# Mix of a spectral layer: block stores on GpSimd's queue, weights alone on SyncE's, part of x loaded later, first spectrum loaded in two parts

## The chip, the cores and the metric

The kernel runs on one core of a Trainium2 chip. The metric is the device time of one execution in microseconds (us). The core has five engines that run their own instruction streams: TensorE (PE, with its weight loads as PEld), VectorE (DVE), ScalarE (ACT), GpSimd (POOL) and SyncE (SP). SP only issues transfers here; ACT and POOL issue some too. All transfers are moved by the core's 16 DMA engines.

## The reference, cut to what matters

The input x is 8 images of 32 channels and 256 by 256 points, in float32. Four layers follow one another, each added to its normalised input: a spectral convolution, a 5 by 5 convolution, a gated recurrence over the columns, and directional running maxima with a 1 by 1 mix. The change concerns the first layer and the start of the second:

```python
x_ft = jnp.fft.rfft2(x)
out_lo = jnp.einsum('bixy,ioxy->boxy', x_ft[:, :, :M1H, :M2H], w1)
out_hi = jnp.einsum('bixy,ioxy->boxy', x_ft[:, :, -M1H:, :M2H], w2)
...
out = jnp.fft.irfft2(out_ft, s=(h, w))
return out + bias
...
x = x + _L0_conv_ref(_gn(x), ...)
x = x + _L1_conv_ref(_gn(x), L1_conv_kernel, 1, 2)
```

Only 32 row frequencies at each end and 32 column frequencies are kept. Each kept mode has its own complex 32 by 32 matrix between channels; multiplying by it is called the Mix here.

## The kernel before, in words

The program has four stages in order of time: `forward_and_mix` (forward transform to 212 us, Mix to about 273 us), `inverse_and_conv` (to about 956 us), `recurrence` (to about 2410 us) and `maxima_and_mix` (to the end). The order of instructions on each engine is the order in which the program writes them; nothing reorders them.

**Mix.** The loop runs over eight blocks q of four row modes each (`NQ` = 8, `KC` = 4). A block uses two weight tiles of 1 MB (c = 0, 1). There are sixteen such loads in all; they use seven buffers (`AHEAD` = 7), so the first seven are loaded during the forward transform and each of the other nine is issued on SP after the half block that frees its buffer (`load_weights`, L109). Per block TensorE does 128 matmuls into PSUM (`mp`, L285, four buffers for each half s), and ACT (s = 0, L298) and DVE (s = 1, L296) copy them into a stage tile `sm`, two buffers for each half. Each block is then stored to a DRAM scratch `smd` by eight DMAs of 64 KB (L307), issued in turn by SP and POOL. In block q = 5, ahead of that block's stores on SP, the six loads of `xb` for the first unit are issued (call at L302, DMA at L323): three parts i of three column tiles each, two channels halves, 768 KB each.

**Waits on the queues.** SP and POOL issue in order. A DMA signals its landing on one of eight semaphores, taken in turn: SP and ACT share eight, POOL has eight of its own. Before a semaphore is used again the DMA that used it last must have landed, so at most eight are in flight for each set.

**Inverse transform and convolution.** A unit is one image and half its channels. `load_spectrum(b)` reads the modes of image b back from `smd` into `spec`: partitions 0 to 63 as stored (L391), 64 to 127 with real and imaginary parts exchanged (L393, two DMAs). For image 0 these three go out on SP, ACT and POOL; image 1's follow on SP; images 2 to 7 are loaded by ACT during the convolution. One part of the exchanged half is negated (image 0: `half`, ACT at L649, 64 partitions x 1024; image 1: DVE at L398; the later ones: POOL). `means` (L404) and `spectrum` (L411 to L421, a chain of small DVE operations) correct the mean. Then `over_rows` does the row matmuls (`tp`, L442, copied by ACT at L449), `over_columns` the column matmuls (`up`, L459), and DVE adds the input `xb` (L468) to give `x1`. A unit has nine column tiles p; p = 0 to 2 use part 0 of `xb`, 3 to 5 part 1, 6 to 8 part 2. The parts of the next unit are loaded by POOL as each part has been used. The 5 by 5 convolution (`vp`, L530) works in place on `x1`, which is stored to `x2d` by twelve DMAs on SP per channel group (L586 to L593). The recurrence reads `x2d`; its first column block is loaded into `first` by POOL and normalised into `xn`.

**Memory.** Tile pools are laid one behind the other from the left, or from the right with `side="right"`. `xb` is in `a2x` on the right; `spec` is in `a2f`, the first pool of `inverse_and_conv` on the left. A new tile waits for the last users of the bytes that it takes over.

Of the kernel before, what the change touches and what calls it, by code (L numbers as in the profile page):

```python
# [9 lines left out]
F32 = mybir.dt.float32  # L10
AF = mybir.ActivationFunctionType
# [5 lines left out]
P = 128  # L17
B, C, H, W = 8, 32, 256, 256
NG = 16
KM = 32  # L20
# [4 lines left out]
Q = H // A  # L25
# [54 lines left out]
def forward_and_mix(tc, k, d, smd, xmean, keep):  # L80
# [4 lines left out]
    nc = tc.nc  # L85
    CH = 4
    NK = C // CH
    HB = H // 32
    KC = 4
    AHEAD = 7  # L90
    SLICES = 4
    HW = float(H * W)
    with ExitStack() as ctx:
# [19 lines left out]
        with ExitStack() as inner:  # L113
# [8 lines left out]
            xs, ys, sps, squares, turned = {}, {}, {}, {}, {}  # L122
# [144 lines left out]
                nc.vector.tensor_copy(xmean, xm)  # L267

        xp2 = keep.enter_context(tc.tile_pool(name="a2x", bufs=1, side="right", reuse_waits="tile"))
        xb = conv_x(nc, d, xp2)  # L270
        sp = ctx.enter_context(tc.tile_pool(name="ms", bufs=2, reuse_waits="tile"))
        ps = ctx.enter_context(tc.tile_pool(name="mp", bufs=4, space=PSUM))
        with tc.manual_schedule(engines=None):
            for q in range(NQ):
                stage = [sp.tile([P, KC, KY, C], F32, name=f"sm_{q}_{s}", tag=f"sm{s}") for s in range(2)]
                for c in range(2):
                    wt = wts.pop(2 * q + c)
                    for i in range(0, KY // 2, 4):
                        mps = [ps.tile([P, 4, KC, C], F32, name=f"mp_{q}_{c}_{i}_{s}", tag=f"mp{s}") for s in range(2)]
                        for y in range(4):  # L280
                            for h in range(2):
                                for s in range(2):
                                    r, to = slice(64 * s, 64 * s + 64), slice(64 * h, 64 * h + 64)
                                    ky = KY * h + KY // 2 * c + i + y
                                    nc.tensor.matmul(  # L285
                                        mps[s][to, y].rearrange("p j o -> p (j o)"),
                                        lhsT=xf[r, ky, q].rearrange("p r b x -> p (r b x)"),
                                        rhs=wt[r, h, i + y].rearrange("p j o -> p (j o)"),
                                        start=True,
                                        stop=True,  # L290
                                    )
# [12 lines left out]

                for s in range(2):
                    for m in range(KC):
                        (nc.sync, nc.gpsimd)[m % 2].dma_start(  # L307
                            out=smd[s, KC * q + m].rearrange("h r b y o -> (h r b) (y o)"),
                            in_=stage[s][m::KC, m].rearrange("p y o -> p (y o)"),
                        )  # L310

    return xb


def conv_x(nc, d, pool):
    CH = 8
    parts = {}

    def load(u, b, h, i, queue):
        lo, hi = 3 * i, 3 * i + 3  # L320
        for ch in range(2):
            t = pool.tile([P, hi - lo, CH, Q], F32, name=f"xb_{u}_{ch}_{i}", tag=f"xb{ch}{i}")
            queue.dma_start(  # L323
                out=t.rearrange("p t c q -> p (t c q)"), in_=d["xl"][b, 2 * h + ch, :, lo * CH * Q : hi * CH * Q]
            )
            for p in range(lo, hi):
                parts[u, ch, p] = t[:, p - lo]

    load.parts = parts
    return load  # L330


# [1 line left out]
    return x2d[b, lo:hi].rearrange("w a c q -> (a c) w q")  # L334


def inverse_and_conv(tc, k, d, smd, xmean, x2d, stb, first, xb):

# [5 lines left out]
    nc = tc.nc  # L344
    CH = 8
# [6 lines left out]
    PLACES = (1, 2, 3, 5, 6, 7, 8)  # L352
    FIRST = (1, 3, 4, 7)
    with ExitStack() as ctx:
        spp = ctx.enter_context(tc.tile_pool(name="a2f", bufs=2, reuse_waits="tile"))
        wk = ctx.enter_context(tc.tile_pool(name="a2w", bufs=2, reuse_waits="tile"))
        one = ctx.enter_context(tc.tile_pool(name="a2c", bufs=1, reuse_waits="tile"))
        sm = ctx.enter_context(tc.tile_pool(name="a2s", bufs=3, reuse_waits="tile"))
        ps = ctx.enter_context(tc.tile_pool(name="a2p", bufs=1, space=PSUM))

        bias = k.bias
# [8 lines left out]
        xs, specs, state = xb.parts, {}, {}  # L370

        def x1_of(u, ch):
            return x1s[(2 * u + ch) % 5][0]
# [10 lines left out]

        def load_spectrum(b):

            t = spp.tile([P, 2, 2, KM // 2, C], F32, name=f"spec_{b}", tag="spec")
            queues = (nc.sync, nc.scalar, nc.gpsimd) if b == 0 else 3 * (nc.scalar if b > 1 else nc.sync,)
            modes = smd[:, :, :, :, b].rearrange("s x h r y o -> (s x) h r (y o)")
            flat = t.rearrange("p h r y o -> p h r (y o)")  # L390
            queues[0].dma_start(out=flat[0:64].rearrange("p h r n -> p (h r) n"), in_=modes.rearrange("p h r n -> p (h r) n"))  # L391
            for ro in range(2):
                queues[ro + 1].dma_start(out=flat[64:128, :, ro], in_=modes[:, :, 1 - ro])  # L393
            specs[b] = t

        def turn(b, engine):
            t = specs[b]
# [245 lines left out]

        n = len(units)
        with tc.manual_schedule(engines=None):
            load_spectrum(0)
            load_spectrum(1)
            half = specs[0][64:128, :, 1]
            nc.scalar.activation(half, half, AF.Copy, scale=-1.0)  # L649
            spectrum(0, means(0))  # L650
            for u in range(2):
                begin(u)
# [553 lines left out]
@with_exitstack  # L1206
def kernel(ctx: ExitStack, tc: tile.TileContext, d: dict, out: bass.AP):
    pool = ctx.enter_context(tc.tile_pool(name="const", bufs=1))
    dram = ctx.enter_context(tc.tile_pool(name="scratch", bufs=1, space=DRAM))
    k = load_consts(tc, pool, d)  # L1210
    xmean = pool.tile([P, B, NG], F32, name="xmean")
    mean1 = pool.tile([P, B], F32, name="mean1")
    mv3 = pool.tile([P, B, 2], F32, name="mv3")
    loaded = recurrence_weights(tc, pool, d)
    keep = ExitStack()
    smd = dram.tile([2, KM, 2, 2, B, KM // 2, C], F32, name="smd")
    x2d = dram.tile([B, W, A, C, Q], F32, name="x2d")
    x3d = dram.tile([W // 8, P, A, 2, 8 * Q], F32, name="x3d")
    fwd = dram.tile([W // 8, P, A, 2, 8 * Q], F32, name="fwd")
    xb = forward_and_mix(tc, k, d, smd, xmean, keep)  # L1220
# [4 lines left out]
    inverse_and_conv(tc, k, d, smd, xmean, x2d, stb, first, xb)  # L1225
# [124 lines left out]
```

## Time and profile before

| | us |
|---|---|
| runs shown | 2980.09, 2985.53, 2977.58 |
| median | 2980.09 |
| profiled execution, its own time | 2983.02 |
| profiled execution, span | 2981.2 |
| forward transform, 0 to 212 | 212 |
| Mix to the first spectrum's load, 212 to 273.5 | 61.5 |
| load of the first spectrum to the first row matmul | about 9 |
| inverse transform and convolution | about 673 |
| recurrence | about 1454 |
| maxima and mix | about 571 |

In the profile, times are counted from the start of the span. A row of the chain of waits or of the timeline gives start, duration and what ran, with the line of the kernel; "x4" means four instructions merged. `SPq`, `ACTq` and `POOLq` are the engines' issuing parts. "DMA smd<-sm" in the chain is a wait until such a transfer landed. In a row of one tile, "536/537/589" are the shortest, median and longest duration in ns. Over the whole span TensorE is busy 93%, DVE 86%, ACT 63%, POOL 30%.

### The profile page before, as it was taken

The numbers are of one execution on the slowest core, as the hardware profiler recorded it, in microseconds if no ns is written. First come the engines' busy times: TensorE is split into PE (matmuls) and PEld (weight loads), VectorE is DVE, ScalarE is ACT, GpSimd is POOL, SyncE is SP. The second block draws the span as 40 slices with busy tenths as digits, with TensorE's granted clock in tenths as the row PEclk, the third lists the DMA queues.
The fourth block names the chain that finished last, engine by engine and source line by source line (L and its number), as shares of the span: only waits on it lengthen the run. The fifth ranks groups of instructions, "written<-read, shape, count | busy, mean of one in ns | idle before, by whom it ended". The sixth has DMA issues, their size and how long they took to land.

```text
span 2981.2 us, 109664 instructions
## 1 busy us (share of the span) xinstructions
PE 2763.3 (93%) x46712; PEld 1633.7 (55%) x46712; DVE 2572.6 (86%) x5130; ACT 1888.7 (63%) x4469; POOL 885.0 (30%) x1266
## 2 busy tenths in 40 slices
PE   8985999999998999999999999999999588888887
PEld 4663454444444666666666666666666233333333
DVE  5762888888887799999999999999999999999998
ACT  4552677677766788888888888888887222222222
POOL 0012111222212555555555555555555200000000
PEclk9997999999999999999999999999999799999998
DMA  9987677777765766676667666766674698888885
GB/s 396 364 308 254 216 228 229 223 232 229 235 220 150 153 144 140 149 172 145 140 146 172 147 141 145 169 153 139 142 168 117 210 376 324 326 324 323 327 337 229
DMA packets 426331, 651.38 MB, mean 218 GB/s; under 512 B 279249, under 2 KB 283233, under 8 KB 399089
## 3 DMA queue, kind: packets, MB, share of 16 engines
q1 hardware_dynamic: 397760, 488.68, 57.2%
q0 software_dynamic: 14928, 75.72, 7.4%
q10 hardware_dynamic: 13152, 79.96, 7.0%
q8 instruction: 366, 6.00, 0.8%
q14 instruction: 125, 1.02, 0.1%
HBM read 371.63 MB, written 272.63 MB: 216 GB/s over the span
## 4 chain that ended last, share of the span: by engine, by line
PE 71%; DVE 20%; DMA 3%; issue 2%; ACT 1%; SPq 1%; POOL 0%; ACTq 0%; DVEq 0%; POOLq 0%
PE r L815 14%; PE z L815 13%; PE vp L530 13%; PE ni L815 7%; PE nh L815 6%; PE up L459 5%; DVE rv L1101 4%; PE yp L142 3%; DVE dq L1116 3%; DVE uq L1118 2%; PE tp L442 2%; DVE m L1127 2%; DVE m L1124 2%; DVE m L1121 2%; PE sp L169 2%
## 5 line engine op out<-in xcount | busy, mean ns | idle before, releaser
L823 PE MATMUL z<-hs,weights 64*64 64x256 f32 x4080 | 538.8, 382 | 0.0
L907 POOL TENSOR_TENSOR xw<-xw,hs 128x256 f32<-128x256 f32 x496 | 339.6, 685 | 633.4 <-DVE hs L906 630.2
L823 PE MATMUL ni<-hs,weights 64*64 64x256 f32 x4080 | 524.9, 375 | 0.0
L823 PE MATMUL r<-hs,weights 64*64 64x256 f32 x4080 | 524.9, 375 | 0.0
L1159 ACT ACTIVATE ot<-o,bres 128x512 f32<-128x512 f32 x256 | 154.9, 688 | 492.1 <-PE o L1133 477.1
L563 DVE SCALAR_TENSOR_TENSOR x<-vp,r,x 128x128 f32<-128x128 f32 (+2 forms) x640 | 350.4, 562 | 96.6 <-PE vp L530 85.6
L530 PE MATMUL vp<-x,c_conv 64*64 64x384 f32 (+5 forms) x4608 | 422.7, 491 | 0.4 <-DVE x L563 0.4
L897 ACT ACTIVATE n<-n,bih 128x256 f32<-128x256 f32 x510 | 259.2, 508 | 183.9 <-DVE n L896 183.9
L899 POOL TENSOR_TENSOR a<-zm,xn 128x256 f32<-128x256 f32 x510 | 372.5, 730 | 3.4 <-ACT zm L892 3.3
L815 PE MATMUL r<-hs,weights 64*64 64x256 f32 x2040 | 319.1, 389 | 1.4 <-DVE hs L906 0.2
L815 PE MATMUL z<-xn,weights 64*64 64x256 f32 x2040 | 305.6, 376 | 9.9 <-ACT xn L795 9.9
L530 PEld LDWEIGHTS vp<-x,c_conv 64*64 64x64 f32 x4608 | 222.3, 132 | 167.8 <-issue 88.9
L1133 PE MATMUL o<-m,wsc 32*32 32x512 f32 x3072 | 224.6, 712 | 95.9 <-DVE m L1127 94.8
L815 PE MATMUL nh<-xn,weights 64*64 64x256 f32 x2040 | 305.7, 377 | 0.0
L815 PE MATMUL r<-xn,weights 64*64 64x256 f32 x2040 | 305.5, 376 | 0.0
L815 PE MATMUL z<-hs,weights 64*64 64x256 f32 x2040 | 305.2, 376 | 0.0
L815 PE MATMUL ni<-hs,weights 64*64 64x256 f32 x2040 | 304.8, 375 | 0.0
L795 ACT ACTIVATE xn<-xw,shift,turned 128x256 f32<-128x256 f32 x492 | 288.5, 586 | 0.0
L823 PEld LDWEIGHTS ni<-hs,weights 64*64 64x64 f32 x4080 | 284.7, 133 | 0.3
L891 DVE SCALAR_TENSOR_TENSOR n<-nh,bhh,rs 128x256 f32<-128x256 f32 x510 | 246.1, 483 | 42.9 <-ACT rs L890 28.9
L823 PEld LDWEIGHTS r<-hs,weights 64*64 64x64 f32 x4080 | 281.1, 131 | 0.2
L890 ACT ACTIVATE rs<-r,brz 128x256 f32<-128x256 f32 x510 | 241.3, 473 | 58.6 <-PE r L823 38.0
(176 smaller groups left out, 6230.5 us busy)
## 6 DMA issues: line engine op xcount, KB each, us to landing
xb<-in_xl_dram POOLq DMA_DIRECT2D x90, 768.0 KB, 7.1
xa<-in_xt_dram SPq DMA_DIRECT2D x64, 1024.0 KB
fwd<-fm SPq DMA_DIRECT2D x256, 256.0 KB
out_dram<-ot ACTq DMA_DIRECT2D x64, 1024.0 KB
xw<-x2d SPq DMA_DIRECT2D x248, 256.0 KB
fw<-fwd SPq DMA_DIRECT2D x31, 2048.0 KB
x3d<-xw SPq DMA_DIRECT2D x240, 256.0 KB
x<-x3d SPq DMA_DIRECT2D x30, 2048.0 KB
```

The source lines that it names most:

```text
L530: ins = nc.tensor.matmul(vps[bank][to, :, dst], lhsT=k.conv[r, P : P + 64] if kind == 2 else k.conv[r, o], rhs=pair_of(u, ch, g, lo, hi, s ...
L563: nc.vector.scalar_tensor_tensor(x, src[o], r1[rows, g : g + 1], x, ALU.mult, ALU.add, accum_out=s1[rows, 0, n, ch, g : g + 1])
L795: nc.scalar.activation(norms[bi][:, b, w], raws[bi][:, b, w], AF.Identity, bias=shift[:, b : b + 1], scale=sc[:, 1, b : b + 1])
L815: ins = nc.tensor.matmul(out[r], lhsT=weights[r, kind, gate, :], rhs=src[r], start=start, stop=stop)
L823: ins = nc.tensor.matmul(out[pairs[1 - i]], lhsT=weights[r, kind, gate, :], rhs=prev[r, :, q0 : q0 + Q], start=False, stop=stop,)
L890: rs = nc.scalar.activation(r, p["r"], AF.Sigmoid, bias=brz[:, 0:1])
L891: nc.vector.scalar_tensor_tensor(m, p["nh"], bhh[:, 2:3], r, ALU.add, ALU.mult)
L897: nc.scalar.activation(m, m, AF.Tanh, bias=bih[:, 2:3])
L899: product = nc.gpsimd.tensor_tensor(a, zm, cur, ALU.mult)
L907: nc.gpsimd.tensor_tensor(raw, raw, new, ALU.add)
L1133: nc.tensor.matmul(banks[bi][b2][i][32 * j : 32 * j + 32].rearrange("p (w q) -> p w q", q=Q), lhsT=wsc[q, b2, t, :], rhs=src[j][q, b2], st ...
L1159: nc.scalar.activation(ot[:, i], banks[bi][b2][i], AF.Identity, bias=bres[:, b2, i : i + 1])
```

## The change

All stores of blocks 0 to 6 are issued by POOL. Those of the last block go to SP, POOL, ACT and SP by row mode. `xb`'s part 0 alone is loaded in the Mix, by SP in block q = 6; part 1 is loaded by POOL behind the late spectrum, part 2 by POOL at the start of `inverse_and_conv`, from a pool of its own (`a2y`). The spectrum's pool moves to the right side, and a function `spectra` loads a chosen range of row modes of one half s with three DMAs. For image 0 the first 24 of 32 modes (`EARLY`) are loaded by SP in block 6, ahead of that block's stores in the program; the other eight after the last block, as stored on SP, exchanged on POOL. Every later image takes six DMAs, three for each half, where it took three. The negation of image 0 is done half by ACT, half by DVE, and DVE's half stands ahead of the `spectrum` chain. In `inverse_and_conv`, `load(0, 2)` (part 2 of `xb`) stands ahead of image 1's spectrum.

```diff
-        xb = conv_x(nc, d, xp2)
+        xb = conv_x(nc, d, [xp2, xp2, None])
+        spp = keep.enter_context(tc.tile_pool(name="a2f", bufs=2, side="right", reuse_waits="tile"))
+        spectrum_of = spectra(nc, smd, spp)
+        EARLY = slice(0, KC * (NQ - 2))
...
-                if AHEAD + 2 * q in (2 * NQ, 2 * NQ + 1):
-                    for i in range(3):
-                        xb(0, 0, 0, i, nc.sync)
+                if q == NQ - 2:
+                    xb(0, 0, 0, 0, nc.sync)
+                    for early in range(2):
+                        spectrum_of(0, early, EARLY, (nc.sync,))
+                queues = 4 * (nc.gpsimd,) if q < NQ - 1 else (nc.sync, nc.gpsimd, nc.scalar, nc.sync)
                 for s in range(2):
                     for m in range(KC):
-                        (nc.sync, nc.gpsimd)[m % 2].dma_start(
+                        queues[m].dma_start(
...
+            for late in range(2):
+                spectrum_of(0, late, slice(EARLY.stop, KM), (nc.sync, nc.gpsimd))
+            xb(0, 0, 0, 1, nc.gpsimd)
+
+    return xb, spectrum_of
+
+
+def spectra(nc, smd, pool):
+    tiles = {}
+
+    def load(b, s, x, queues):
...
+        if b not in tiles:
+            tiles[b] = pool.tile([P, 2, 2, KM // 2, C], F32, name=f"spec_{b}", tag="spec")
+        modes = smd[s, x, :, :, b].rearrange("x h r y o -> x h r (y o)")
+        flat = tiles[b].rearrange("p h r y o -> p h r (y o)")
+        own, other = (slice(64 * i + KM * s + x.start, 64 * i + KM * s + x.stop) for i in range(2))
+        queues[0].dma_start(out=flat[own].rearrange("p h r n -> p (h r) n"), in_=modes.rearrange("p h r n -> p (h r) n"))
+        for ro in range(2):
+            queues[-1].dma_start(out=flat[other, :, ro], in_=modes[:, :, 1 - ro])
...
-            t = pool.tile([P, hi - lo, CH, Q], F32, name=f"xb_{u}_{ch}_{i}", tag=f"xb{ch}{i}")
+            t = pools[i].tile([P, hi - lo, CH, Q], F32, name=f"xb_{u}_{ch}_{i}", tag=f"xb{ch}{i}")
...
-        spp = ctx.enter_context(tc.tile_pool(name="a2f", bufs=2, reuse_waits="tile"))
...
+        xb.pools[2] = ctx.enter_context(tc.tile_pool(name="a2y", bufs=1, reuse_waits="tile"))
...
-            t = spp.tile([P, 2, 2, KM // 2, C], F32, name=f"spec_{b}", tag="spec")
-            queues = (nc.sync, nc.scalar, nc.gpsimd) if b == 0 else 3 * (nc.scalar if b > 1 else nc.sync,)
...
+            queue = nc.scalar if b > 1 else nc.sync
+            for s in range(2):
+                spectrum_of(b, s, slice(0, KM), (queue,))
...
-            load_spectrum(0)
+            load(0, 2)
             load_spectrum(1)
-            half = specs[0][64:128, :, 1]
-            nc.scalar.activation(half, half, AF.Copy, scale=-1.0)
+            for y in range(2):
+                half = specs[0][64:128, y, 1]
+                if y:
+                    nc.vector.tensor_scalar_mul(half, half, -1.0)
+                else:
+                    nc.scalar.activation(half, half, AF.Copy, scale=-1.0)
             spectrum(0, means(0))
```

More of the change, by code (lines that the diff above doesn't have):

```diff
@@ L310, in forward_and_mix, with conv_x @@
                         )
-    return xb
-def conv_x(nc, d, pool):
+            for late in range(2):
[13 more added lines that the diff above has]
+            queues[-1].dma_start(out=flat[other, :, ro], in_=modes[:, :, 1 - ro])
+    load.tiles = tiles
+    return load
+def conv_x(nc, d, pools):
     CH = 8
@@ L327, in load @@
                 parts[u, ch, p] = t[:, p - lo]
-    load.parts = parts
+    load.parts, load.pools = parts, pools
     return load
@@ L334, in columns, with inverse_and_conv @@
     return x2d[b, lo:hi].rearrange("w a c q -> (a c) w q")
-def inverse_and_conv(tc, k, d, smd, xmean, x2d, stb, first, xb):
+def inverse_and_conv(tc, k, d, xmean, x2d, stb, first, xb, spectrum_of):
     nc = tc.nc
@@ L369, in inverse_and_conv @@
         units = [(b, h) for b in range(B) for h in range(C // (2 * CH))]
-        xs, specs, state = xb.parts, {}, {}
+        xs, specs, state = xb.parts, spectrum_of.tiles, {}
         def x1_of(u, ch):
@@ L385, in load_spectrum @@
         def load_spectrum(b):
-            t = spp.tile([P, 2, 2, KM // 2, C], F32, name=f"spec_{b}", tag="spec")
-            queues = (nc.sync, nc.scalar, nc.gpsimd) if b == 0 else 3 * (nc.scalar if b > 1 else nc.sync,)
[L389 to L394, printed above, removed]
+            queue = nc.scalar if b > 1 else nc.sync
+            for s in range(2):
+                spectrum_of(b, s, slice(0, KM), (queue,))
         def turn(b, engine):
@@ L1219 @@
     fwd = dram.tile([W // 8, P, A, 2, 8 * Q], F32, name="fwd")
-    xb = forward_and_mix(tc, k, d, smd, xmean, keep)
+    xb, spectrum_of = forward_and_mix(tc, k, d, smd, xmean, keep)
     rest = ExitStack()
@@ L1224 @@
     first = later.tile([P, B, 8, Q], F32, name="first")
-    inverse_and_conv(tc, k, d, smd, xmean, x2d, stb, first, xb)
+    inverse_and_conv(tc, k, d, xmean, x2d, stb, first, xb, spectrum_of)
     keep.close()
```

## The prediction

> **What bounds the kernel now.** The chain of waits for the whole span says PE 71%, DVE 20%, DMA 3%: from the convolution on, the end is set by TensorE, one step after another. So whatever brings the convolution's first matmul forward brings the end forward by the same amount, if nothing later eats it. The change sits ahead of that matmul. I therefore read the chain cut to 190 to 320 us, then SP's queue, then the landing of the stores.
>
> The chain, in order of time (start, duration, what):
>
> ```profile
> 211.96 10.28 PE mp L285 x282
> ...
> 222.69 10.07 DMA wt<-in_wm_dram
> ...
> 235.15 9.02 DMA wt<-in_wm_dram
> ...
> 244.19 7.62 DMA smd<-sm
> ...
> 253.38 13.77 DMA smd<-sm
> ...
> 274.38 7.08 DMA spec<-smd
> ...
> 281.47 1.06 ACT spec L649
> ...
> 282.58 6.48 PE tp L442 x32
> ```
>
> From 222 us on the Mix is not TensorE's: it hangs on weights landing, then on stores of its own blocks. One store alone holds it 13.77 us. Between the last block stored (273.38) and the first row matmul (282.58) lie 9.2 us: spectrum load, sign pass, little else. SP's queue shows why a store took so long:
>
> ```profile
> 247.83 4.84 SPq L323 DMA_DIRECT2D xb<-in_xl_dram  x6
> 252.78 18.99 SPq L307 DMA_DIRECT2D smd<-sm  x12
> 273.75 1.25 SPq L391 DMA_DIRECT2D spec<-smd  x2
> 275.03 1.39 SPq L393 DMA_DIRECT2D spec<-smd  x2
> ```
>
> Six xb loads of 768 KB (4.7 MB) are issued ahead of the last twelve SP stores. TensorE's matmuls for Mix end near 257 us and nothing runs for 10 us. The windows (PE, PEld, DVE, ACT, POOL busy, clock, DMA share, GB/s) show the transfer engines full meanwhile, then empty:
>
> ```profile
> 255.00:260.00 5.00, 2.21 (x82) 1.96 (x71) 0.23 (x1) 0.00 (x0) 1.39 (x3) 1.00 1.02 414
> 260.00:265.00 5.00, 0.00 (x0) 0.00 (x0) 0.00 (x0) 0.00 (x0) 0.00 (x0) 0.59 0.85 332
> 265.00:270.00 5.00, 0.00 (x0) 0.00 (x0) 2.37 (x4) 2.05 (x4) 0.33 (x1) 0.50 0.13 48
> ```
>
> Last, the GpSimd stores alone, first block (beside weights) and last block (alone):
>
> ```profile
> L307 POOL DMA_DIRECT2D smd<-sm x4: 536/537/589, 218.9 to 220.5; - x4
> DMA to landing us min/median/max: 6.1/6.6/6.9
> ...
> L307 POOL DMA_DIRECT2D smd<-sm x4: 536/537/538, 269.7 to 271.3; - x4
> DMA to landing us min/median/max: 1.8/1.9/1.9
> ```
>
> An issue costs 0.54 us of POOL; a store lands after 6.1 to 6.9 us in traffic, 1.9 us without. Over the Mix the landings of the POOL stores lie between 5.6 and 7.5 us until 256 us.
>
> **What the Trainium skill says.** "DMA: Bandwidth & Descriptors", section "Issuing engines are not separate DMA queues": transfers issued by SP, ACT and GpSimd share the same 16 engines, and another issuer saves only issue time. The trace agrees: the share stands near 1.0 from 220 to 260 us whichever queue issues. So the new queue gives no bandwidth; what can be won is order. Section "Queues, rings and completion order": each engine takes turns between the queues that have work. That is why a store on another queue need not wait for megabytes ahead of it on SP's, and why it still takes 6.5 us instead of 1.9 beside them. "TensorE: Matmul & The Clock Gate", Part 1: an idle TensorE falls to half clock. Here the granted clock goes 0.59, 0.50 after 260 us, and the first 32 row matmuls take 6.48 us.
>
> **The change, part by part.**
>
> 1. *Bytes.* Before, Mix moves 9 weight loads of 1 MB (9.4 MB), 64 stores of 64 KB (4.2 MB) and 4.7 MB of xb: 18.3 MB. After: one third of xb (1.6 MB) and three quarters of the first spectrum (0.8 MB of 1.05) beside the same weights and stores: 16 MB. The 3.1 MB that leave are worth 8 us at 400 GB/s. They are loaded after the late spectrum, and must land before the columns that use them: p=3 is added 12.6 us after the first row matmul (295.2 against 282.58), p=6 17.5 us after. Issued on POOL 2 to 4 us ahead of that matmul, beside the second spectrum, they need about 5 us (1 MB at the 204 to 216 GB/s that the windows show for spectra) + 4 + 4 us of DMA time. That leaves some 7 us to spare: cost 0. The cover is the row matmuls, copies and first columns, 8.3 us from 282.58 to the first add at 290.90.
>
> 2. *Weights alone on SP.* They no longer wait behind stores, only for their buffer (seven, freed by TensorE). By the pace of step 3 the last is issued at about 238 us, against 242.6, and has landed by 244; xb's third follows at once.
>
> 3. *All stores on POOL.* Eight per block are 8 x 0.54 = 4.3 us of issue, a little more than TensorE's 4.2 us for 128 matmuls. The built program adds one wait: from the ninth store on, each waits for the landing of the store eight before it. Behind the waiting store stand only stores, so blocks follow each other at one landing time, L. Nobody but the evictions (two buffers per half) waits for them. First issue 218.6 (end of ACT's fourth eviction). With L = 6.7: blocks 1, 2, 3 at 225.3, 232.0, 238.7. Weights and xb end near 246, so from block 4 (245.2) landing falls towards 2 to 3 us and the step becomes issue plus eviction (2.5 us for DVE's four): blocks 5 and 6 at 249.5 and 253.8; block 7's stores, on three queues, 258 to 260. All landed at **262** against 273.4: 11.4 us. Bounds for this unknown: if L never falls, block 7's two POOL stores land at 219.2 + 8L = 272.8, a gain of 0.6; if only bytes counted (16 MB at 400 GB/s from 217), about 257, a gain of 16. I take 262, because the same stores did land in 1.9 us once nothing else moved.
>
> 4. *Spectrum in two parts.* The early part waits for block 5's stores, on SP, where only block 7's four stores stand behind it (about 257.5): hidden by block 7's evictions. The late part is a quarter: 2 issues on SP, 4 on POOL at 0.62 us, so the last is out 2.1 us after the last landing. Before, the load took 8.1 us (273.38 to 281.45). I take 2.1 + 3 = 5.1 us; between 4.0 (an unhindered 1.9 us landing) and 9.2 (the old 7.1 us). By the same page, section "Why a DMA increments its semaphore by 16 and not by 1", a load over 8 partitions uses at most 8 engines; no trace here shows it, and it is part of that upper bound. Gain **3.0** (-1.1 to 4.1).
>
> 5. *Sign pass.* ACT's 1.05 us becomes about 0.55 (half the columns), but DVE's half stands ahead of its mean chain. DVE: 0.35 (half of its 0.69 us turn at 323.4), wait for y0 (0.6), then 1.1 us to L420, which the row matmuls read: 1.8 us instead of 1.1. Loss **0.7** (0.3 to 0.9).
>
> 6. *Later.* Each later spectrum is six DMAs instead of three. On ACT that is 3 x 0.65 = 2 us, six times; ACT stands idle 4.35 us before the next copy of tp each time, less the last issue: free, at worst 1 us each if a DMA semaphore is not yet free. The moved pools put the recurrence's first xn block over a conv buffer whose twelve stores are issued by 959 us; xn starts at 968.7 behind statistics: 0. DVE's fm, which now waits for a DMA at 977.96 (0.40 us), no longer does: 0 to 0.4.
>
> Sum: 11.4 + 3.0 - 0.7 = **13.7 us**. The profiled execution took 2983.02 us, 1.8 more than its span; it becomes 2969.3. It stands 2.9 above the median of 2980.09, so the median becomes **2966.4 us**. A measurement of this kernel tells about 0.3% (8.9 us) from no change.
>
> **The rivals.**
>
> *Only bytes count.* Landing on the POOL queue is shorter than 6.7, evictions never wait, and Mix ends with its traffic at 257: about 18.7 us, 2961.4. For it: SP's ring holds fewer transfers ahead. Against: every landing read in traffic was 5.6 or more.
>
> *The store queue stays slow.* Eight stores now share the queue where four did. If L stays at 6.7 to 7.3 through the last block (xb's third and the early spectrum keep the engines full), the last landing is 272.8 to 277.6, and with steps 4 and 5 the result is 2.9 us less to 1.9 us more: about 2977 to 2982, no change. For it: 5.7 us even beside xb alone at 254 us. Against: only 1.6 MB of xb now follows the weights, and the early part is issued only once block 5 has landed.
>
> *Slower.* The same queue, past its tipping point: each store's landing grows with eight outstanding. Within a block of four it grew from 6.1 to 6.9. 219.2 + 8L exceeds 273.4 + 2.3 + 8.9 from L = 8.2 on; at 8.5 it ends at 287.2, 11.5 us later: about 2991.6. It needs 8.2 us in all eight blocks, with traffic that ends near 246.
>
> **How the numbers follow.** Forecast 0.68; only bytes 0.12; slow queue 0.15; slower 0.05. Of the forecast's share nearly all lies above 8.9 us (its own range, the last landing within 3 us of 262 and step 4 at 2 to 4.1, is 10 to 18). So faster by over 0.3%: 0.79; within: 0.16; slower: 0.05. The range 2959 to 2976 takes in the bytes case and the upper edge of the forecast, and leaves out most of the slow queue and the slower case.
>
> **What would show it.** The first L442 matmul near 269 us instead of 282.6; no idle stretch like 257 to 267 in Mix; POOL stores in steps of 6 to 7 us until block 4 and then about 4.3; the last landing near 262; spectrum landed 5 us later; every row from the convolution on shifted by one constant. It is wrong if the step between blocks stays above 6 us to the end, if the late part lands after 7 us or more, or if DVE's adds for p=3 or p=6 wait for xb.

## The result, and the profile after

| | before | after | difference |
|---|---|---|---|
| median, first set (16 runs each) | 2980.93 us | 2974.92 us | ratio 0.9981, 95% interval 0.9974 to 0.9987: 5.7 us less (3.9 to 7.8) |
| median, another set (12 and 6 runs) | 2983.69 | 2974.50 | ratio 0.9970, 0.9958 to 0.9981 |
| profiled execution, its own time | 2983.02 | 2974.03 | -8.99 |
| span | 2981.2 | 2972.2 | -9.0 |
| last Mix store landed | 273.36 | 265.60 | -7.76 |
| first spectrum landed, sign pass starts | 281.47 | 272.83 | -8.64 |
| first row matmul (`tp`) | 282.58 | 274.44 | -8.14 |
| first convolution matmul (`vp`) | 305.85 | 297.23 | -8.62 |

The change makes the kernel faster by 0.2%, less than the 13.7 us that were forecast; the median is 8.5 us above the forecast, near the upper end of the range. The gain lies under the 0.3% that the prediction took for the limit of what can be told, a case to which it gave 0.16; with 16 runs of each kernel the interval still excludes no change. The profiled executions overstate the gain by 3 us: that of before was 2.1 us slower than its median, that of after 0.9 faster.

The chain of waits after, cut to the Mix (start, duration, what):

```profile
219.60 5.54 DMA smd<-sm
...
231.03 6.61 DMA smd<-sm
...
237.93 6.33 DMA smd<-sm
...
247.87 6.07 DMA smd<-sm
...
256.06 3.57 DMA smd<-sm
...
262.22 0.52 SPq L310
...
262.78 2.82 DMA smd<-sm
...
267.79 1.12 POOL spec L335 x2
```

The waits on weights have gone from the chain, and so has the stall of 13.77 us. In their place stands what the prediction said: each block waits for the landing of an earlier block's stores, 5.5 to 6.6 us. But these waits last to 254 us, longer than forecast, and the prediction fails there and in what follows. The issues of POOL and SP there (start, duration, what, and in brackets what the engine waited for):

```profile
245.38 0.54 POOL L310 DMA_DIRECT2D smd<-sm  x1 [0.30 <-issue]
246.14 3.35 POOL L310 DMA_DIRECT2D smd<-sm  x6 [0.22 <-issue]
250.02 0.54 POOL L310 DMA_DIRECT2D smd<-sm  x1 [0.54 <-DMA smd<-sm]
251.69 2.17 POOL L310 DMA_DIRECT2D smd<-sm  x4 [1.13 <-DMA smd<-sm]
254.46 6.96 POOL L310 DMA_DIRECT2D smd<-sm  x13 [0.60 <-DMA smd<-sm]
262.63 0.54 POOL L310 DMA_DIRECT2D smd<-sm  x1 [1.22 <-DVE sm L299]
266.47 2.43 POOL L335 DMA_DIRECT2D spec<-smd  x4 [3.30 <-DMA smd<-sm]
```

```profile
216.16 24.82 SPq L109 DMA_DIRECT2D wt<-in_wm_dram  x9
241.09 0.89 SPq L349 DMA_DIRECT2D xb<-in_xl_dram  x2
255.67 0.96 SPq L333 DMA_DIRECT2D spec<-smd  x1
256.69 1.56 SPq L335 DMA_DIRECT2D spec<-smd  x2
259.75 0.76 SPq L333 DMA_DIRECT2D spec<-smd  x1
260.55 1.55 SPq L335 DMA_DIRECT2D spec<-smd  x2
262.22 2.44 SPq L310 DMA_DIRECT2D smd<-sm  x4
265.87 2.38 SPq L333 DMA_DIRECT2D spec<-smd  x3
```

POOL issues eight stores for each block, so they can be counted off: the one at 250.02 is the last of block 4. Block 5 starts at 251.69, 6.3 us after block 4 (245.38), and block 6 with the fifth of the thirteen that start at 254.46, at 256.60, another 4.9 us later; for both steps 4.3 us were forecast. From 254.46 on POOL issues without a gap, 0.54 us each: the step really becomes the issue time, but later than forecast, only from block 6 on. On SP the second half of the early spectrum waits for block 5's last store (issued at 256.06, landed at 259.63, chain), and block 7's four SP stores stand behind its three issues, until 262.22. Two of these four were ready at 259.8, when ACT had made its last copy.

The windows of after (PE, PEld, DVE, ACT, POOL busy, clock, DMA share, GB/s):

```profile
240.00:245.00 5.00, 2.33 (x88) 2.09 (x78) 0.87 (x2) 2.13 (x4) 3.13 (x6) 1.00 1.02 401
245.00:250.00 5.00, 4.78 (x120) 4.78 (x124) 2.00 (x5) 1.52 (x3) 3.84 (x8) 0.66 1.01 412
250.00:255.00 5.00, 4.43 (x148) 3.90 (x140) 2.75 (x5) 2.69 (x6) 3.23 (x7) 1.00 0.61 236
```

The transfer engines are full until 250, not 246. Block 4's stores, issued from 245.38 on, took 4.5 to 6.1 us to land, where 2 to 3 were forecast.

### The profile page after: what moved, and what is told of

It is laid out like the page before. It is cut to its first block, busy times and chain, and to the rows that moved or that the text cites. A ratio compares the mean times of both kernels' runs of the same rounds, so it can differ in the third digit from the quotient of the medians.

```text
span 2972.2 us, 109713 instructions
## 1 busy us (share of the span) xinstructions
PE 2762.5 (93%) x46712; PEld 1634.2 (55%) x46712; DVE 2573.2 (87%) x5131; ACT 1889.5 (64%) x4469; POOL 906.2 (30%) x1299
## 4 chain that ended last, share of the span: by engine, by line
PE 71%; DVE 20%; issue 3%; DMA 3%; ACT 1%; SPq 1%; POOL 1%; DVEq 0%; ACTq 0%; POOLq 0%
PE r L840 14%; PE vp L551 13%; PE z L840 13%; PE ni L840 7%; PE nh L840 6%; PE up L480 4%; DVE rv L1126 4%; PE yp L142 3%; DVE dq L1141 3%; DVE uq L1143 2%; DVE m L1152 2%; DVE m L1149 2%; DVE m L1146 2%; PE sp L169 2%; PE tp L463 2%
## 5 line engine op out<-in xcount | busy, mean ns | idle before, releaser
L922 ACT ACTIVATE n<-n,bih 128x256 f32<-128x256 f32 x510 | 259.2, 508 | 184.3 <-DVE n L921 184.3
```

The source lines that it names most:

```text
L922: nc.scalar.activation(m, m, AF.Tanh, bias=bih[:, 2:3])
```

## The experiments

The landmarks of each profile in one table. "Landed" is the last Mix store, from the chain or from the first issue that waits for it; "load" runs from there to the sign pass, "sign" from there to the first row matmul. Executions of one kernel lie up to 5.3 us from their median, and one profile is one execution: 1 us between two profiles decides nothing. The medians come from four sets, each with its own runs of before (2980.93, 2981.96, 2981.57 and 2983.69 us), so between sets the ratios are to be compared; after again, sign_act, xb_last again and all_late are of one set.

| kernel | landed | load | sign | first `tp` | first `vp` | median (runs) | ratio to before, 95% |
|---|---|---|---|---|---|---|---|
| before | 273.4 | 8.1 | 1.11 | 282.58 | 305.85 | 2980.93 (16) | |
| before again | 273.9 | 8.4 | 1.11 | 283.42 | 305.28 | 2981.43 (1) | |
| after | 265.6 | 7.2 | 1.61 | 274.44 | 297.23 | 2974.92 (16) | 0.9981 (0.9974 to 0.9987) |
| after again | 268.6 | 6.7 | 1.61 | 276.95 | 299.04 | 2974.50 (6) | 0.9970 (0.9958 to 0.9981) |
| xb_later | 264.2 | 8.0 | 1.11 | 273.31 | 296.63 | 2971.24 (5) | 0.9966 (0.9953 to 0.9978) |
| queue_only | 268.4 | 8.2 | 1.11 | 277.62 | 300.03 | 2978.12 (21) | 0.9985 (0.9979 to 0.9992) |
| split_stores | 266.6 | 7.2 | 1.61 | 275.39 | 298.55 | 2976.05 (14) | 0.9979 (0.9971 to 0.9987) |
| late_alone | 266.0 | 5.8 | 1.89 | 273.69 | 295.47 | 2974.40 (6) | 0.9972 (0.9961 to 0.9984) |
| no_early | 265.7 | 7.5 | 1.61 | 274.84 | 296.75 | 2974.10 (7) | 0.9974 (0.9963 to 0.9984) |
| stage3 | 264.5 | 7.0 | 1.72 | 273.20 | 295.72 | 2973.32 (6) | 0.9971 (0.9960 to 0.9983) |
| sign_act | 267.2 | 7.1 | 1.10 | 275.39 | 297.83 | 2974.85 (7) | 0.9971 (0.9959 to 0.9982) |
| xb_last | 259.8 | 8.0 | 1.10 | 268.83 | 290.96 | 2972.36 (5) | 0.9964 (0.9950 to 0.9977) |
| xb_last again | 263.0 | 7.9 | 1.10 | 272.00 | 294.68 | 2968.56 (5) | 0.9953 (0.9940 to 0.9965) |
| all_late | 264.6 | 6.0 | 1.96 | 272.55 | 294.66 | 2974.59 (5) | 0.9968 (0.9955 to 0.9980) |

### Both kernels once more

Unchanged kernels; before:

> The kernel before, unchanged, for a second profile of it. Theory A (the shift seen between the two profiles, 8.1 us at the first row matmul, is typical): its first row matmul again starts within 1 us of 282.6 us and its last Mix store lands within 1 us of 273.4. Theory B (the first profile of before caught a slow Mix, which is why the profiles differ by 9.0 us and the medians by 6.0): the first row matmul starts 2 to 4 us earlier, at 279 to 280.

After:

> The changed kernel once more, to see whether its first profile is typical. Open is why the first profile shows the first convolution matmul 8.6 us and the end of the span 9.0 us earlier, while the medians differ by 6.0 us. Theory A (the Mix repeats, the rest of the span varies by a few us from run to run): first row matmul within 1 us of 274.4, first convolution matmul within 1.5 us of 297.2, the difference of the medians lies in what follows. Theory B (the first profile was a lucky Mix): first row matmul at 276 to 278, first convolution matmul at 299 to 300.

Before repeats within 1 us up to the convolution. After does not: its Mix ended 3 us later in the second profile, and the first convolution matmul came at 299.04, not 297.23. So the first profile of after was a somewhat lucky Mix; the second execution took 2978.83 us, the slowest of its six. The gain at that matmul is 6 to 9 us, which agrees with both sets of medians. From `vp` to the end of the span the two profiles of after take 2675.0 and 2678.0 us, those of before 2675.4 and 2674.3: whether up to 3 us are given back there in some executions, two profiles can't tell.

### The deferral of xb alone: xb_later

```diff
# against before
-                if AHEAD + 2 * q in (2 * NQ, 2 * NQ + 1):
-                    for i in range(3):
-                        xb(0, 0, 0, i, nc.sync)
+                if q == NQ - 2:
+                    xb(0, 0, 0, 0, nc.sync)
...
+            load(0, 1)
+            load(0, 2)
```

> The kernel before with one part of the change alone: two thirds of xb moved out of the Mix (part 0 in block 6 on SP, parts 1 and 2 behind the first spectrum on POOL); stores still in turn on SP and POOL, spectrum in one piece. Theory A (the 4.7 MB of xb ahead of the SP stores was the whole gain, the queue of the stores hardly matters): the last Mix store lands near 266, the first row matmul starts near 275 (load 8.1, sign 1.1), time about 6 us under before. Theory B (stores behind the weights on SP hold the Mix just as much): the last store lands at 269 to 271, first row matmul at 278 to 280, time 2 to 4 us under before.

The stores still alternate between SP and POOL, and still the landing comes at 264.2, as early as with the whole change. SP's queue and the chain's end:

```profile
253.30 1.07 SPq L322 DMA_DIRECT2D xb<-in_xl_dram  x2
256.68 5.86 SPq L306 DMA_DIRECT2D smd<-sm  x8
```

```profile
249.60 9.98 PE mp L285 x254
261.95 2.25 DMA smd<-sm
264.87 7.31 DMA spec<-smd
```

The landmarks come somewhat earlier than theory A had them. Part 2 is in the pool `a2y`, as in the change. Only 1.6 MB stand ahead of SP's last stores. The Mix then ends with two blocks of matmuls in a row, not with a stall. The deferral alone is worth about 10 us (ratio 0.9966): all of the change's gain.

### The queue move alone: queue_only

```diff
# against before
-                        (nc.sync, nc.gpsimd)[m % 2].dma_start(
+                        (4 * (nc.gpsimd,) if q < NQ - 1 else (nc.sync, nc.gpsimd, nc.scalar, nc.sync))[m].dma_start(
```

> The kernel before with the other part alone: all stores of blocks 0 to 6 on POOL, the last block's on SP, POOL, ACT and SP; all of xb still in the Mix on SP in block 5, spectrum in one piece. Theory A (bytes and order of xb are the gain; POOL's queue of eight in flight is no faster than two queues): the six xb loads stand beside the stores instead of ahead of them, landing of the POOL stores stays near 6 us through block 6, last store at 270 to 273, first row matmul 279 to 282, time 0 to 3 us under before. Theory B (the queue is the gain): last store near 266, first row matmul near 275, time 6 us under before.

The chain, with all 4.7 MB of xb still in the Mix:

```profile
238.10 6.41 DMA smd<-sm
...
244.79 6.36 DMA smd<-sm
...
251.44 6.38 DMA smd<-sm
...
261.10 2.14 DMA smd<-sm
```

The stall of 13.77 us goes here too, since no store stands behind xb on POOL, but its blocks follow at 6.4 us each to the end of the traffic. Its windows show DMA share 1.01 to 1.03 from 240 to 260. The landing (268.4) and the first row matmul (277.62) lie between the two theories. The move is worth 4.5 us (ratio 0.9985, 0.9979 to 0.9992), where the deferral is worth 10. It moves the same bytes in another order: the Trainium skill's "DMA: Bandwidth & Descriptors", section "Issuing engines are not separate DMA queues", says that another issuer saves only issue time; what this run won is the wait behind xb, a gain of order that the sentence does not cover.

### The whole change with the old split of stores: split_stores

```diff
# against after
-                queues = 4 * (nc.gpsimd,) if q < NQ - 1 else (nc.sync, nc.gpsimd, nc.scalar, nc.sync)
+                queues = 2 * (nc.sync, nc.gpsimd) if q < NQ - 1 else (nc.sync, nc.gpsimd, nc.scalar, nc.sync)
```

> The changed kernel with one part undone: the stores of blocks 0 to 6 in turn on SP and POOL as before; xb, early spectrum and sign pass as changed. Theory A (queue worth little): last Mix store 265 to 267, first row matmul 274 to 276, time within 1.5 us of the changed kernel. Theory B (queue is the gain): SP's stores wait again for weights on the shared semaphores, last store at 269 to 271, first row matmul 278 to 280, time 4 to 6 us over the changed kernel, near before.

Landing 266.6 and ratio 0.9979: not to be told from after, as theory A said. With xb deferred the queue move brings nothing more; the two are remedies for one stall and do not add up. But two opposite effects hide in that equality. DVE's last copies, first after, then this run:

```profile
259.85 2.48 DVE L299 COPY sm<-mp 128x512 f32<-128x512 f32 x4 [2.68 <-DMA smd<-sm]
```

```profile
256.16 0.69 DVE L299 COPY sm<-mp 128x512 f32<-128x512 f32 x1 [0.18 <-PE mp L288]
```

In after DVE stood until block 5's last store had landed and ended at 262.33. With stores on two queues it waited for nothing but TensorE and ended at 256.85. The other profiles with xb deferred divide in the same way: DVE's last copy ends at 256.1 to 260.3 in the four whose stores alternate (this one, xb_later, xb_last twice), and at 261.0 to 264.8 in the six with all stores on POOL and two stage buffers. (xb's part 0 went out at 252.5 here and at 241.1 in after; but all_late, with no xb in the Mix at all, ends its copies at 261.0 and xb_last at 256.1 and 259.2.) So with xb out of the way the single queue of stores holds the copies back. What this run won there it lost on SP's queue:

```profile
257.39 3.02 SPq L335 DMA_DIRECT2D spec<-smd  x2
261.16 5.43 SPq L310 DMA_DIRECT2D smd<-sm  x8
```

All eight of SP's last stores, of blocks 6 and 7, wait behind the early part until 261.16, and the last landing comes 9.7 us after DVE's last copy; in the two profiles of xb_last, with nothing but stores on SP, it comes 3.7 and 3.8 us after.

### The early spectrum left out: no_early

```diff
# against after
-                    for early in range(2):
-                        spectrum_of(0, early, EARLY, (nc.sync,))
...
-                spectrum_of(0, late, slice(EARLY.stop, KM), (nc.sync, nc.gpsimd))
+                spectrum_of(0, late, slice(0, KM), (nc.sync, nc.gpsimd))
```

> The changed kernel without the early part: image 0's whole spectrum is loaded after the Mix, by the same two queues (two DMAs on SP, four on POOL). Theory A (the early part brings little: it delays the last block's stores on SP and adds traffic to the tail, and a quarter of the spectrum takes nearly as long as all of it): last store lands at 264 to 265, the load takes 8 to 9 us, first row matmul within 1.5 us of the changed kernel's 274.4, time the same within 1.5 us. Theory B (as predicted, the early part is worth 3 us): last store 265.6, load 10 us, first row matmul at 277 to 278, time 3 us over the changed kernel.

The whole spectrum is loaded after the Mix. From the last landing on it takes 7.5 us, the quarter 7.2; the first row matmul comes 0.4 us later, the first convolution matmul 0.5 us earlier, the median is 2974.10 (ratio 0.9974). So loading three quarters early brought nothing that these runs can see. The load is not as short as 7.5 us, though. POOL's share of it:

```profile
264.41 1.12 POOL L333 DMA_DIRECT2D spec<-smd  x2 [0.52 <-issue]
266.27 1.06 POOL L333 DMA_DIRECT2D spec<-smd  x2 [0.74 <-DMA smd<-sm]
```

Its first half goes out 1.3 us ahead of the last landing (265.70), since SP, free of the early part, sent the first of its last four stores at 260.65 instead of 262.22. From the first issue to the sign pass the whole takes 8.8 us, the quarter in after 7.0 (265.87 to 272.83). The early part thus shortened the load by 1.8 us, but the load began 1.5 us later.

### A third stage buffer: stage3

```diff
# against after
-tag=f"sm{s}") for s in range(2)]
+tag=f"sm{s}", bufs=2 + s) for s in range(2)]
```

Part 1 of xb moves to the pool `a2y`, issued at the start of `inverse_and_conv`, to make room.

> The changed kernel with three stage buffers instead of two for the half that DVE copies (xb's part 1 moves to the pool of part 2 to make room and is issued at the same place). In the changed kernel DVE waits 22 us in all for stores of two blocks before. Theory A (the stage buffers pace the blocks): last store 2 to 4 us earlier, at 262 to 263.5, first row matmul at 271 to 272.5. Theory B (POOL's queue, eight stores in flight, paces them; the copies only follow): DVE's wait goes, POOL's wait for landings grows, last store within 1 us of 265.6.

Who waited for the stores, first after, then this run (us, times):

```profile
  DVE sm L299: 22.2, 5
...
  POOL smd L310: 8.7, 11
  ACT sm L301: 7.1, 2
```

```profile
  ACT sm L301: 22.6, 5
  DVE sm L299: 13.1, 4
  POOL smd L310: 8.7, 9
```

The third buffer spared DVE 9.1 us of waiting and ACT, with its two, waited 15.5 us more. DVE's last copy ended at 258.16 instead of 262.33, but the landing came only 1.1 us earlier, within the spread, and POOL's wait did not grow as theory B had it: neither theory fits whole. POOL still had stores to issue until 261.2, and SP's four stood behind the early spectrum until 260.44. So a third buffer for one engine lets its copies finish earlier and does not by itself end the Mix earlier; three for both halves were not tried.

### The late part without other traffic: late_alone

```diff
# against after
-            xb(0, 0, 0, 1, nc.gpsimd)
...
-            load(0, 2)
-            load_spectrum(1)
...
+            for i in (1, 2):
+                xb(0, *units[0], i, nc.scalar)
...
+                if p == 2:
+                    load_spectrum(1)
```

ACT issues the two parts behind its sign pass, and image 1's spectrum goes out on POOL after the third column tile.

> The changed kernel with the transfers behind the late spectrum moved away from it: image 1's spectrum is issued by POOL after column tile 2 of the first unit, xb's parts 1 and 2 by ACT after its sign pass. The changed kernel took 7.2 us from the last Mix store's landing (265.6) to the late part's (272.8). Theory A (contention: the late part shares the DMA engines with image 1's spectrum and xb): last store unchanged at 265.6, the late part lands after 5 us, first row matmul near 272, time 1.5 to 2.5 us under the changed kernel unless adds wait for xb. Theory B (the four issues on POOL, 2.4 us, behind a 0.9 us start, set it): the late part again takes about 7 us, first row matmul at 274 to 274.5, no change.

The load takes 5.8 us instead of 7.2; the first row matmul is 0.8 us earlier, the first convolution matmul 1.8 us. The late load takes 6.7 to 7.2 us in the five profiles with the traffic issued right behind it (image 1's spectrum and xb's parts 1 and 2) and 5.8 and 6.0 in the two with less (this run and all_late). So 0.7 to 1.4 us of step 4's miss are that traffic. The median (2974.40, ratio 0.9972) does not show it.

### The sign pass undivided: sign_act

```diff
# against after
-            for y in range(2):
-                half = specs[0][64:128, y, 1]
-                if y:
-                    nc.vector.tensor_scalar_mul(half, half, -1.0)
-                else:
-                    nc.scalar.activation(half, half, AF.Copy, scale=-1.0)
+            half = specs[0][64:128, :, 1]
+            nc.scalar.activation(half, half, AF.Copy, scale=-1.0)
```

> The changed kernel with the sign pass of image 0 undivided on ACT, as before. Theory A (the split costs what the profile shows, since DVE's half stands ahead of its mean chain): from the spectrum's landing to the first row matmul 1.1 us instead of 1.6, and the end earlier by 0.5 us at most, too little for the medians to tell. Theory B (the split is worth its half of ACT's pass): 2.0 us instead of 1.6.

From landing to the first row matmul it takes 1.10 us as before, against 1.61 in both profiles of after: theory A. The timelines of after's ACT, DVE and PE show the reason:

```profile
272.83 0.63 ACT L674 ACTIVATE spec<-spec 64x512 f32<-64x512 f32 x1 [13.05 <-DMA spec<-smd]
```

```profile
272.83 0.42 DVE L672 TENSOR_SCALAR spec<-spec 64x512 f32<-64x512 f32 x1 [10.49 <-DMA spec<-smd]
273.28 0.19 DVE L432 TENSOR_TENSOR yb<-y,bias 128x32 f32<-128x32 f32 x1
...
274.26 0.16 DVE L442 COPY stb<-m 128x32 f32<-128x32 f32 x1
```

```profile
274.44 5.98 PE L463 MATMUL tp<-c_eh,spec 128*64 128x256 f32 x32 [2.11 <-DVE stb L442]
```

ACT's half ends at 273.46, but the row matmuls wait for DVE, whose mean chain starts only behind its own half and ends at 274.42. The split costs 0.5 us, too little for the medians to tell.

### All of xb after the first spectrum: xb_last, twice

```diff
# against before
-                if AHEAD + 2 * q in (2 * NQ, 2 * NQ + 1):
-                    for i in range(3):
-                        xb(0, 0, 0, i, nc.sync)
...
-            load_spectrum(1)
+            for i in range(3):
+                load(0, i)
...
+                if p == 2:
+                    load_spectrum(1)
```

Stores alternate as before; the first spectrum's load and the sign pass are as before; image 1's spectrum is issued by POOL.

> The kernel with xb alone moved (stores in turn on SP and POOL, spectrum in one piece on three queues, ACT's sign pass), taken further: all three parts of xb are issued by POOL behind the first spectrum, and image 1's spectrum by POOL after column tile 2. Theory A (traffic ahead of the last stores and beside the first spectrum is what costs): last store at 260 to 262 against 264.2 with part 0 still in the Mix, spectrum landed 5 us later, first row matmul at 266 to 268.5, time 4 to 6 us under that kernel, near 2966. Theory B (the store queue itself paces the Mix, or xb comes late for column tile 0): last store at 263.5 or later, or DVE's first add waits for xb; time within 1.5 us of 2971.

> The kernel before with all of xb loaded after the first spectrum and image 1's spectrum later, once more. Theory A (every us won ahead of the first row matmul reaches the end): first convolution matmul within 1 us of 291.0, median 2966 to 2970, some 5 us under the changed kernel in the same set. Theory B (part of it is given back later): the same landmarks, but a median of 2971 to 2974, within 3 us of the changed kernel.

The last stores of the second profile, with nothing but stores on SP:

```profile
242.23 19.18 SPq L304 DMA_DIRECT2D smd<-sm  x16
263.25 0.60 SPq L389 DMA_DIRECT2D spec<-smd  x1
```

```profile
250.00:255.00 5.00, 5.00 (x140) 5.00 (x144) 3.72 (x7) 2.36 (x6) 2.14 (x4) 0.74 0.34 123
255.00:260.00 5.00, 3.40 (x126) 3.16 (x114) 3.45 (x5) 2.88 (x5) 2.81 (x6) 1.00 0.31 110
```

Between 250 and 260 the transfer engines are a third busy and TensorE works: the Mix ends when its own work ends. The first adds did not wait for xb: DVE's first is at 279.73, behind the `up` matmul. Of the first run's expectations the landmarks came out near theory A (landed 259.8, first row matmul 268.83), but not the time: its median, 2972.36, lies level with xb_later's (ratios 0.9964 and 0.9966), so that taking part 0 out of the Mix too is not shown to be worth anything at the end. Of the second run's expectations the landmark missed by 3.7 us (294.68, not 291.0), since the Mix varies here too; that profile was the slowest execution of its five. The median of 2968.56 us is 5.9 under after in the same set, and its slowest run (2971.82) stands level with after's fastest (2971.81). So xb_last beats both kernels: ratio to before 0.9953 (0.9940 to 0.9965), in the other set 0.9964 (0.9950 to 0.9977).

### The whole change with all of xb deferred: all_late

```diff
# against after
-                    xb(0, 0, 0, 0, nc.sync)
...
-            xb(0, 0, 0, 1, nc.gpsimd)
+            for i in range(2):
+                xb(0, 0, 0, i, nc.gpsimd)
...
-            load_spectrum(1)
...
+                if p == 2:
+                    load_spectrum(1)
```

> The changed kernel with the rest of xb also taken out of Mix: parts 0 and 1 behind the late spectrum on POOL, image 1's spectrum on POOL after the third column tile. Theory A (the queues and the deferral are two remedies for one stall and don't add up; the short late load wins only without traffic beside it): last landing 259 to 262, as with the deferral alone, the late load 4.5 to 6, first row matmul 265 to 269. Theory B (they add up: with weights alone beside the stores the last landing falls by another 4 us): last landing near 256, first row matmul near 262.

Both theories missed: landed at 264.6, not 259 to 262 nor 256, and the first row matmul at 272.55 lies above both. The load did shrink to 6.0 us, as in late_alone. DVE's timeline and SP's queue name what holds the landing:

```profile
258.50 2.48 DVE L299 COPY sm<-mp 128x512 f32<-128x512 f32 x4 [3.49 <-DMA smd<-sm]
```

```profile
259.20 1.55 SPq L335 DMA_DIRECT2D spec<-smd  x2
260.87 2.43 SPq L309 DMA_DIRECT2D smd<-sm  x4
```

DVE's last copies waited 3.49 us for an earlier block's store on POOL's queue, though TensorE had only its last matmuls left (to 257.7); and block 7's four SP stores stood behind the early spectrum until 260.87. Had SP been free, the two of ACT's half would have been out before and the last issue come some 1.1 us earlier (two issues of 0.54). The rest points to the single queue of stores, as split_stores does; how the delay divides between the two was argued, not tried. The median, 2974.59, stands level with after and 6.0 us above xb_last in the same set. The two profiles don't show that difference: their first convolution matmuls are level (294.66 and 294.68), because all_late was caught in one of its fastest executions and xb_last in its slowest. Alternating stores with an early part on a queue that carries no stores was not tried.

## Why the prediction was wrong in size

- **What bounds the kernel: right.** In the first pair of profiles what was won ahead of the first row matmul reached the end: 8.1 us there, 8.6 at the first convolution matmul, 9.0 in the span.
- **Steps 1, 2 and 6: right at a cost of 0.** DVE's adds never waited for xb. But step 2's time for the last weight was too early: its issue ended at 240.98, against 238 forecast, and step 3 built on that. The six-part loads of later spectra do show up as waits of ACT's copies of `tp` (21.3 us in four waits), but from the first convolution matmul to the last statistics matmul before the recurrence both kernels take the same time: 654.4 us before (305.85 to 960.26), 654.45 after (297.23 to 951.68).
- **Step 3: the mechanism right up to block 4, the gain 3.6 us too large** (landed at 265.6, not 262). Two terms failed. First, "Weights and xb end near 246, so from block 4 (245.2) landing falls towards 2 to 3 us": the traffic ended at 250. The step's own byte count said so: 9.4 MB of weights, 1.6 of xb and 2.1 of the stores of blocks 0 to 3 are 13.1 MB, 33 us at 400 GB/s, from 217 to 250. Blocks 1 to 4 started at 225.7, 232.1, 238.9 and 245.4, as forecast, but block 4's stores landed in 5.7 us (median), so block 5 started at 251.69, not 249.5, and block 6 at 256.60, not 253.8: 2.8 us. (By the step's own 6.7 us block 4 would be at 245.4, not 245.2; the slip changes nothing.) Second, "block 7's stores, on three queues, 258 to 260": DVE's last evictions (259.85 to 262.33) waited for block 5's landing at 259.63, and SP's four stores went out from 262.22 on, behind the early spectrum, where a free SP would have had two left. The remaining 0.8 us lie there. The step let only the evictions wait for the stores and took that wait to end with the traffic; in after it lasts to the last block (DVE's 2.68 us), and with alternating stores it is gone (split_stores). Step 4 had called the early part hidden by block 7's evictions; nearly: it holds two stores that were ready. In no_early, without it, the last landing comes 2.6 us after DVE's last copy, in after 3.3.
- **Step 4: wrong, 7.2 us instead of 5.1.** Both terms were too small. The last issue was out 3.3 us after the last landing (0.9 to POOL's first issue, 2.4 for its four), not 2.1; and the last of the loads landed 3.9 us behind its issue, not 3. The 7.2 us in all are above the 7 us which the prediction named as a sign of being wrong (6.7 in the second profile). late_alone recovers up to 1.4 us by keeping image 1's spectrum and xb away. That a quarter would be much faster than the whole was the wrong idea: from its first issue the whole takes 8.8 us in no_early, the quarter 7.0 in after. Why the last landing takes 3.9 us for so few bytes stays open: that a load over 8 partitions is spread over few engines, which the step put into its upper bound, no run tested.
- **Step 5: right.** 0.5 us lost; forecast 0.7, within 0.3 to 0.9; sign_act gives it back.
- **The sum** at the first row matmul: 7.8 + 0.9 - 0.5 = 8.1 us measured (rounded), 13.7 forecast. 3.6 of the difference are step 3, 2.1 step 4, and 0.2 came back in step 5. The medians fell by only 6.0 us (5.7 by the ratio); the 2 us between that and the 8.1 are no term of the sum, but the choice of executions: the prediction carried the offset of one profile of before over to after, and the first profile of after was a lucky Mix. The second ends its Mix 3 us later, with step 3 that much further off.
- **The rivals.** "Only bytes count" fell: of the stores issued before 250 us none landed in less than 4.5 us. "The store queue stays slow" was half right, its landings stayed near 6 us one block longer than forecast, but not to the end. "Slower" fell: no store took more than 7.4 us in the first profile of after, 8.4 in the second, where it needed 8.2 in every block; and its reading that the landing "grew from 6.1 to 6.9" within a block had the order wrong, since of those four stores the first landed in 6.95 us and the last in 6.12. The rival that was missing is the one the runs found: the queue move and the deferral remove the same 13.77 us stall, so the deferral alone does as well as both (xb_later), and with all of xb deferred the kernel without the queue move and the early part is 6.0 us faster than with them (xb_last against all_late; the split sign pass can be 0.5 us of that).

## What to carry to other kernels

Where a store stands behind megabytes of loads that nobody needs yet, move those loads out of the stage first; a new queue for the stores is a second remedy for the same stall, and the two gains are not to be added. One queue for all stores has a price of its own: here, once the loads were out of the way, it held back the copies that fill the stage buffers. Before a load is put early onto a queue, look at what stands behind it there: here it held stores that were ready, and leaving it out cost nothing. Price a transfer behind a dependency by its issues and its last landing, not by its bytes alone: here 3.3 us and 3.9 us for a quarter of the bytes.

## What the runs showed of the hardware that was not expected

- A quarter of the spectrum (0.26 MB) takes nearly as long to load as the whole (1.05 MB): 6.7 to 7.2 us from the last landing, against 7.9 to 8.4 in the versions with three loads; in no_early the whole takes 8.8 us from its first issue, the quarter in after 7.0. With less traffic beside it the quarter takes 5.8 to 6.0 us.
- The same kernel's Mix ends up to 3 us apart in two executions (265.6 and 268.6 after, 259.8 and 263.0 in xb_last), while the two of before lie within 0.6 us. In the second profile of after the delay is there by 254 us: the last stores of blocks 2 and 3, for which the stores of the next blocks wait, landed in 7.7 and 6.6 us instead of 6.3 and 5.2. What slowed these two, the runs don't show.
